# Sorted rows requested three tiles ahead, projection and norm as separate steps, and a walk that ends six experts sooner, in an attention-and-experts kernel

## The chip, the cores and the metric

The kernel runs on 1 core of one Trainium2 chip. The metric is device time in microseconds (us), the median of several executions. A core has five engines with a queue of instructions each: TensorE (PE in the profile), VectorE (DVE), ScalarE (ACT), GpSimd (POOL) and SyncE (SP). Each takes its instructions in the order in which the program has them, so an instruction that waits holds up all that stand behind it on its engine. DMA transfers are started from the queues of SP, ACT and POOL.

## The reference, cut to what matters

The input x is (2, 1024, 256) in float32. Each row of 256 is normed to xn. Two things are computed from xn, and the output is x plus both.

```
x  = L0_attn_x
xn = _layernorm(x)
out = x + attention(xn) + ffn(xn)

# attention: tokens of 16 channels in a 256 x 64 grid; two branches of 8 channels,
#   windows of 8 in one direction each: softmax(q k / sqrt(8)) v, plus a 3x3 depthwise conv of v
att    = concat(branch0, branch1) @ proj_w + proj_b
normed = (att - mean) * rsqrt(var + 1e-5) * ln_w + ln_b      # over 16 channels
att    = transpose(tokens + normed)

# ffn: 16 experts of 176 hidden units; every one of the 2048 rows goes to 6 of them
logits -> sigmoid -> choice of 2 of 4 groups, then of 6 experts, weights scaled by 2.5
out_row = sum over its 6 experts of  w * (silu(row @ g_e.T) * (row @ u_e.T)) @ d_e.T
          + a shared expert of 352 units
```

## The kernel before

**Stages.** The first 85 us or so load x and the weights, norm the rows (L223 to L249), choose the experts, sort the 2048 rows by which experts they go to, and run the shared expert in between (`shared_steps`, L266). The normed rows, with their 16 weights behind them, lie in DRAM as `xw_d`. The rest of the run interleaves two things.

**The experts.** The sorted rows stand in 16 tiles of 128 (`NTL`). `sorted_tile(t)` (L817) fetches tile t: an indirect DMA on POOL's queue gathers its rows into `xg` (three buffers), TensorE transposes them (L823), ACT copies them to `xsT` (L824), and DVE copies their 16 weights to `wsrt` (L826) and works out the six weights of the tile (L834 to L837). A buffer of `xg` is free again when both the transposes and L826 have read it. Every tile meets six experts, and there are 14 extra lists of rows for pairs that the six don't cover. One expert on one tile is a *slot*, and two slots are a *unit*. A slot's part on the way up (`up`, L851) is two matmuls L855 (four passes in the profile), a Silu on ACT (L857) and a multiply on DVE (L858, `hms`). The product's PSUM tile `pr_u` has three buffers. A unit's part on the way down is three transposes L869, a copy L871, and the matmuls L881 (six experts) or L889 (extras). When a tile's six experts are summed, ACT copies the sum to `ysum` (L1035; extras L1042), and POOL adds its rows to the output by an indirect DMA (L996, a *scatter-add*). There are 30 of these. Because they all add to the same output tensor, each one waits for the transfer before it.

**The attention.** `attention_steps` (L1049) yields its work as steps. There are four blocks (two batches, two halves of the columns), and each has: copies of rows (L670), eight projections (L675, each with four copies on ACT, L677 to L680), four products and sums on DVE (L688, L692), the softmax (L698 to L704), four weighted products and sums (L709, L714), two divides (L722), and eight transposes back (L729) with two copies into `oT` (L731). After the blocks come the last projections and their norms, `attended(g, h, xe, att)` (L765), eight times: four matmuls `pp` (L781), a copy with bias on ACT (L784), four transposes `pa` (L787), square (L791), variance (L793), root (L794), reciprocal (L795), multiply (L796), and on POOL a multiply and two additions into `att` (L797, L802). ACT loads a table for the root and another one for the Silu of the next expert. After each second g, `attention_added` (L1062) adds `att` to the output by four transfers from POOL's queue (L1065).

**What sets the order.** The loop at L1107 goes through the units. In each slot it fetches sorted tiles that are due (L1110), starts an expert, finishes an earlier one, and then calls `walked()` (L1082), which takes steps of the attention as long as they are behind the pace. Each step carries two costs, one for DVE and one for TensorE:

```python
of_slot = {"six": (0.5, 2.0), "extra": (0.8, 2.5)}
END = 72
pace = (whole[0] - LEAD - END * of_slot["six"][0] / of_slot["six"][1]) / (whole[1] - END)
...
while step and done[0] <= pace * done[1]:
    step[2]()
    counted(step)
    last, step = step, next(walk, None)
    if last[1] > 1:
        break
```

`END` is the TensorE time, in these costs, that is to be left when the attention is through. This gives the order in which the program states its work; a scheduling layer below it then moves single instructions within each engine's queue before the program is built.

Of the kernel before, what the change touches and what calls it, by code (L numbers as in the profile page):

```python
# [41 lines left out]
NTL = ROWS // P  # L42
# [9 lines left out]
def csw_block_moe(ctx: ExitStack, tc: tile.TileContext, x, qkv_w, conv_w0, conv_b0, conv_w1, conv_b1,  # L52
# [33 lines left out]
    def by_hl(t):  # L86
        return t.rearrange("(p l) d -> p l d", l=16)
# [135 lines left out]
    def statistics(g):  # L223
        st = small.tile([P, 4, 6], F32, name="st")
        mv = small.tile([P, 4, 2], F32, name="mv")
        for l in range(4):
            nc.vector.bn_stats(out=st[:, l, :], in_=xx[:, 4 * g + l, 0:W])
        for l in range(4):
            nc.vector.bn_aggr(out=mv[:, l, :], in_=st[:, l, :])
        rs = small.tile([P, 4], F32, name="rs")  # L230
        nc.scalar.activation(rs, mv[:, :, 1], AF.Sqrt, bias=eps)
        return mv, rs
# [84 lines left out]
    def meanwhile(until):  # L317

        while spent[1] is not None and spent[0] + spent[1] <= until:
            spent[0] += spent[1]  # L320
            spent[1] = next(share)
# [77 lines left out]
    for g in range(4):  # L399
        now, held = held, statistics(g + 1) if g < 3 else None  # L400
# [361 lines left out]
            nc.vector.tensor_copy(below[:, :, :, 0], pairs[:, 0:4, h, :, 1])  # L762
        return xe

    def attended(g, h, xe, att):  # L765

        if not last_room:
            last_room.extend(work.tile([P, 2, TB], F32, tag="f1024", name=name, bufs=3) for name in ("xr", "a", "sq"))
        xr = last_room[0].rearrange("p l (k d) -> p (l k) d", d=W)
        quarters = [t[:, n] for t in last_room[1:] for n in range(2)]  # L770
        a_, sq_ = quarters[(2 * g + h) % 3], quarters[3]
        if h == 0:
            nc.gpsimd.dma_start(out=xr, in_=by_hl(xw_d[0:ROWS, :])[:, 4 * g : 4 * g + 4, 0:W])

        pp = ps_m.tile([P, 4, P], F32, tag="m", name="pp")
        terms = [(lp[:, 0], xnT[:, h, 4 * g : 4 * g + 4, :]),
                 (lp[:, 1], xnT[:, h, 4 * g - 4 : 4 * g, :] if g > 0 else xe[0][:, h]),
                 (lp[:, 2], xnT[:, h, 4 * g + 4 : 4 * g + 8, :] if g < 3 else xe[1][:, h]),
                 (wp, oT[:, g, h])]
        for n, (l_, r_) in enumerate(terms):  # L780
            nc.tensor.matmul(pp.rearrange("p l q -> p (l q)"), lhsT=l_.rearrange("p t c -> p (t c)"),  # L781
                             rhs=r_.rearrange("p l q -> p (l q)"), start=(n == 0), stop=(n == len(terms) - 1))
        aT = a_.rearrange("p (l q) -> p l q", l=4)
        nc.scalar.activation(aT, pp, AF.Identity, bias=pbc)  # L784
        pa = ps_m.tile([P, 4, P], F32, tag="m", name="pa")
        for l in range(4):
            nc.tensor.transpose(pa[:, l, :], aT[:, l, :], ident)  # L787
        rows_a = pa.rearrange("p l (t c) -> p (l t) c", c=C)
        wide = [P, 32, C]
        sq, a = (t.rearrange("p (n c) -> p n c", c=C) for t in (sq_, a_))  # L790
        nc.scalar.activation(sq, rows_a, AF.Square)  # L791
        var = small.tile([P, 32], F32, tag="var", name="var")
        nc.vector.tensor_reduce(out=var, in_=sq, axis=AX.X, op=ALU.add)  # L793
        nc.scalar.activation(var, var, AF.Sqrt, bias=eps, scale=1.0 / C)  # L794
        nc.vector.reciprocal(var, var)  # L795
        nc.vector.tensor_tensor(a, rows_a, var.unsqueeze(2).to_broadcast(wide), ALU.mult)  # L796
        nc.gpsimd.tensor_tensor(a, a, lw.unsqueeze(1).to_broadcast(wide), ALU.mult)  # L797
        for m in range(2):
            to = att[m].rearrange("p n (l d) -> p n l d", d=16)[:, :, 4 * g : 4 * g + 4, 8 * h : 8 * h + 8]
            one = a.rearrange("p (l t) c -> p c l t", t=8)[:, 8 * m : 8 * m + 8]  # L800
            two = xr.rearrange("p l (t c) -> p c l t", c=C)[:, 8 * m : 8 * m + 8, :, 8 * h : 8 * h + 8]
            nc.gpsimd.tensor_tensor(to, one, two, ALU.add)  # L802
# [11 lines left out]
    w6 = route.tile([P, NTL * TOPK], F32, name="w6")  # L814
    st_ = {}

    def sorted_tile(t):  # L817
        xg = work.tile([P, ROW], F32, tag="xg", name="xg", bufs=3)
        nc.gpsimd.indirect_dma_start(out=xg, out_offset=None, in_=xw_d[:, :],  # L819
                                     in_offset=bass.IndirectOffsetOnAxis(ap=of[:, t : t + 1], axis=0))  # L820
        px_ = ps_m.tile([P, 2, P], F32, tag="m", name="px_")
        for h in range(2):
            nc.tensor.transpose(px_[:, h, :], xg[:, P * h : P * h + P], ident)  # L823
        nc.scalar.copy(xsT[:, t], px_)  # L824
        w = wsrt[:, t]
        nc.vector.tensor_copy(w, xg[:, W:ROW])  # L826

        if t > 1 and t % 2 == 0:
            return
        n = 1 if t < 2 else 2  # L830
        ts = slice(t + 1 - n, t + 1)
        wf = small.tile([P, 2, TOPK, E], F32, tag="wf", name="wf", bufs=1)[:, 0:n]
        wide = [P, n, TOPK, E]
        nc.vector.tensor_tensor(wf, e6b[:, ts].unsqueeze(3).to_broadcast(wide),  # L834
                                row_f.unsqueeze(1).unsqueeze(1).to_broadcast(wide), ALU.is_equal)
        nc.vector.tensor_tensor(wf, wf, wsrt[:, ts].unsqueeze(2).to_broadcast(wide), ALU.mult)
        nc.vector.tensor_reduce(out=w6.rearrange("p (t k) -> p t k", k=TOPK)[:, ts], in_=wf, axis=AX.X, op=ALU.add)  # L837
# [209 lines left out]
    att = []  # L1047

    def attention_steps():  # L1049
        for b in range(B):  # L1050
            for h in range(2):
                yield from attention(b, h)
        xe = []
        yield 0.6, 0.0, lambda: xe.extend(edges())
        att.extend(work.tile([P, 8, W], F32, tag=tag, name="att") for tag in ("prod", "qk"))
        for g in range(4):
            for h in range(2):
                yield 1.4, 3.9, lambda: attended(g, h, xe, att)
            if g % 2:
                waiting.extend([lambda m=m, b=b, n=g // 2: attention_added(m, b, n) for m in range(2) for b in range(B)])  # L1060

# [6 lines left out]

    of_slot = {"six": (0.5, 2.0), "extra": (0.8, 2.5)}
    of_tile = (0.75, 0.25)  # L1070
    END = 72
    in_walk = [4 * (16 * 2.3 + 3.3 + 2.5 + 1.5 + 1.4) + 0.6 + 8 * 1.4, 4 * 6.2 + 8 * 3.9]
    LEAD = 12
    done = [float(-LEAD), 0.0]
    whole = [in_walk[n] + NTL * TOPK * of_slot["six"][n] + NL * of_slot["extra"][n] + NTL * of_tile[n] for n in range(2)]
    pace = (whole[0] - LEAD - END * of_slot["six"][0] / of_slot["six"][1]) / (whole[1] - END)

# [1 line left out]
        for n in range(2):  # L1079
            done[n] += cost[n]  # L1080

    def walked():  # L1082
        step = held_.pop()
        while step and done[0] <= pace * done[1]:
            step[2]()
            counted(step)
            last, step = step, next(walk, None)
            if last[1] > 1:
                break
        held_.append(step)  # L1090

    walk = attention_steps()
    held_ = [next(walk)]
    sorted_tile(0)
    sorted_tile(1)
    walked()
    meanwhile(100)
    tiles_sorted = 2
    laid_out = list(units())
    begun_, hT_ = {}, {}  # L1100
# [6 lines left out]
    for u in range(len(laid_out) + 2):  # L1107
        for q in range(2):
            i = 2 * u + q
            while tiles_sorted < NTL and 5 * (tiles_sorted - 2) <= 6 * (i - 1):  # L1110
                sorted_tile(tiles_sorted)
                counted(of_tile)
                tiles_sorted += 1
            if i in (2, 4, 8) or i >= 14:
                next(extras_ if i < 14 else lists_, None)
            if u + 1 < len(laid_out) and laid_out[u + 1][0] == "extra":
                n = laid_out[u + 1][1] + q
                ahead[n] = gathered(lists[:, n : n + 1])
            if u < len(laid_out):
                if q == 0:  # L1120
                    fetched(u)
                begun_.setdefault(u, []).append(begun(laid_out[u], q, hms[:, u % 2]))
            if q == 1:
                if 0 <= u - 1 < len(laid_out):
                    hT_[u - 1] = hidden(hms[:, (u - 1) % 2])
                if 0 <= u - 2 < len(laid_out):
                    finished(laid_out[u - 2], hT_.pop(u - 2), wts[:, (u - 2) % 3], begun_.pop(u - 2))
            counted(of_slot[laid_out[min(u, len(laid_out) - 1)][0]])
            walked()
            if done_:  # L1130
                to_out(*done_.pop(0))
            while waiting:
                waiting.pop(0)()
# [8 lines left out]
    with tc.For_i(0, count_, 1) as n:  # L1142
# [5 lines left out]
        xg = gathered(to[:, 0:1])  # L1148
# [58 lines left out]
```

## Time and profile before

| | |
|---|---|
| median of the 3 runs | 453.98 us (453.94 to 454.08) |
| the profiled execution | 454.73 us |
| its span, first to last instruction | 453.0 us |
| mean granted TensorE clock | 0.976 |
| TensorE busy | 396.2 us, 87% of the span |
| DVE busy | 292.2 us, 65% |
| ACT busy | 215.2 us, 48% |
| POOL busy | 189.1 us, 42% |
| L855, up matmuls of the sorted rows | 132.0 us, 384 of 476 ns |
| L996, the 30 scatter-adds on POOL | 51.3 us, 1711 ns each |
| L819, the 16 gathers of sorted rows | 19.3 us, 1204 ns each |

How to read it: a row of digits shows the span in 40 slices of 11.3 us, each digit the busy share in tenths (9 is 90% or more). In a timeline a line gives the start, the time, the engine, the line of the kernel, the operation with output and input, and in brackets how long the engine had stood idle before it and what it waited for. The chain of waits follows the run back from its last instruction, at each step to what released it. A busy TensorE is not one at its peak, since the ends of its matmuls are modelled; the clock that it was granted is shown beside it.

### The profile page before, as it was taken

Reading aid. Unit: us, or ns where it says so; the run is one execution under the profiler, and the core shown is the slowest. Engines: PE = TensorE matmul, PEld = TensorE weight load, DVE = VectorE, ACT = ScalarE, POOL = GpSimd, SP = SyncE. Lnnn points to the kernel's source line nnn. Section 1 sums busy time; section 2 is a strip of 40 time slices with the busy share of each in tenths; the row PEclk is TensorE's granted clock in tenths of the full one; section 3 lists DMA queues with packets and bytes.
Section 4 is the critical chain, followed back from the end, with each engine's and each line's share of the span. In section 5 each row is a group of like instructions: output and inputs, shape, how many; then the busy total and the mean of one; then the engine's idle time right before and its main releaser. Section 6 shows DMA issues by size and latency. Waiting matters only on the chain.

```text
span 453.0 us, 6294 instructions
## 1 busy us (share of the span) xinstructions
PE 396.2 (87%) x1668; PEld 248.4 (55%) x1669; DVE 292.2 (65%) x515; ACT 215.2 (48%) x535; POOL 189.1 (42%) x207
## 2 busy tenths in 40 slices
PE   0999999998896978989799979899999899979990
PEld 0445465656464745656566646656666555447670
DVE  4627958689896945899838989469997223331210
ACT  2945248363372337253345363373623657773330
POOL 7300000322335151976832434505436274789331
PEclk9999999999898989999999999999999999998996
DMA  8999841322232100211122234202332101923922
GB/s 235 344 326 308 228 156 34 67 74 32 69 87 44 38 20 6 38 32 31 27 52 44 52 50 70 48 27 40 58 84 60 32 14 56 114 61 71 120 42 24
DMA packets 40178, 37.56 MB, mean 83 GB/s; under 512 B 5300, under 2 KB 37616, under 8 KB 40112
## 3 DMA queue, kind: packets, MB, share of 16 engines
q0 software_dynamic: 11616, 13.52, 18.5%
q1 hardware_dynamic: 27472, 22.59, 16.7%
q10 hardware_dynamic: 1056, 1.05, 0.7%
q8 instruction: 15, 0.25, 0.2%
q14 instruction: 19, 0.16, 0.1%
HBM read 27.70 MB, written 12.45 MB: 89 GB/s over the span
## 4 chain that ended last, share of the span: by engine, by line
PE 40%; DVE 24%; DMA 12%; issue 8%; POOL 7%; ACT 6%; POOLq 0%; SPq 0%; DVEq 0%; ACTq 0%
PE pr_u L855 9%; PE pr_y L881 5%; DVE pv L709 5%; DVE pr L688 4%; DVE s L692 4%; PE pg L275 4%; DMA out_dram<-ysum,lists 4%; PE pp L781 4%; PE py L290 4%; DVE o L714 4%; PE pu L275 4%; DMA out_dram<-att 4%; DVE hms L858 3%; PE pq L675 3%; DMA xg<-xw_d,lists 3%
## 5 line engine op out<-in xcount | busy, mean ns | idle before, releaser
L855 PE MATMUL pr_u<-w1s,xsT 128*128 x384 | 132.0, 476 | 2.4 <-DVE hms L858 1.9
L855 PEld LDWEIGHTS pr_u<-w1s,xsT 128*128 128x128 f32 x384 | 70.5, 193 | 39.0 <-issue 8.2
L996 POOL DMA_INDIRECT out_dram<-ysum,lists x30 | 51.3, 1711 | 88.3 <-ACT ysum L1035 36.1
L857 ACT ACTIVATE sg<-pr_u 128x176 f32<-128x176 f32 x110 | 34.5, 317 | 79.0 <-PE pr_u L855 72.7
L858 DVE SCALAR_TENSOR_TENSOR hms<-sg,w,pr_u 128x176 f32<-128x176 f32 x96 | 36.9, 389 | 44.2 <-ACT sg L857 42.6
L688 DVE TENSOR_TENSOR pr<-qk 128x2048 f32<-128x2048 f32 x16 | 36.6, 2287 | 15.6 <-ACT qk L677 10.9
L709 DVE TENSOR_TENSOR pv<-s,v 128x2048 f32<-128x2048 f32 x16 | 36.6, 2285 | 3.2 <-ACT s L700 3.1
L957 POOL TENSOR_SCALAR ysum<-row_h,spot 128x128 f16<-128x128 f16 x26 | 27.9, 1102 | 25.2 <-PE rows_of L948 15.0
L293 POOL DMA_DIRECT2D out_dram<-ysum x4 | 3.7, 921 | 78.7 <-ACT ysum L291 78.7
L692 DVE TENSOR_REDUCE s<-pr 128x256 f32<-128x2048 f32 x16 | 36.5, 2279 | 0.1
L714 DVE TENSOR_REDUCE o<-pv 128x256 f32<-128x2048 f32 x16 | 36.4, 2274 | 0.0
L869 PE MATMUL ph<-ident,hms 128*128 128x128 f32 x165 | 30.3, 281 | 6.1 <-ACT hT L871 3.6
L869 PEld LDWEIGHTS ph<-ident,hms 128*128 128x128 f32 x165 | 21.8, 145 | 24.1 <-issue 8.0
L982 POOL DMA_INDIRECT xg<-xw_d,lists x14 | 20.1, 1437 | 23.9 <-DVE hms L858 15.5
L881 PE MATMUL pr_y<-w2a,hT 128*128 x96 | 29.1, 386 | 0.0
L881 PE MATMUL pr_y<-wts,hT 128*128 128x256 f32 x96 | 28.9, 384 | 0.0
L881 PE MATMUL pr_y<-w2b,hT 112*128 x96 | 28.9, 382 | 0.0
L855 PE MATMUL pr_u<-w1s,xd 128*128 x56 | 21.4, 507 | 7.3 <-ACT xd L991 7.3
L871 ACT COPY hT<-ph 128x384 f32<-128x384 f32 x55 | 26.4, 480 | 2.1 <-PE ph L869 1.5
L675 PE MATMUL pq<-wq,rows 128*128 128x384 f32 x64 | 24.6, 501 | 3.1 <-ACT oT L731 2.0
L819 POOL DMA_INDIRECT xg<-xw_d,lists x16 | 19.3, 1204 | 18.6 <-PE pr_u L855 6.7
L290 PE MATMUL py<-room 128*128 128x256 f32 x96 | 23.9, 388 | 1.7 <-DVE room L284 1.7
(403 smaller groups left out, 713.1 us busy)
## 6 DMA issues: line engine op xcount, KB each, us to landing
w1s<-in_w_dram SPq DMA_DIRECT2D x22, 256.0 KB
wts<-in_w_dram SPq DMA_DIRECT2D x55, 64.0 KB
wts<-in_w_dram SPq DMA_DIRECT2D x55, 48.0 KB
xw_d<-xx SPq DMA_DIRECT2D x4, 544.0 KB
w2a<-in_w_dram SPq DMA_DIRECT2D x4, 512.0 KB
out_dram<-ysum POOLq DMA_DIRECT2D x4, 512.0 KB
xr<-xw_d POOLq DMA_DIRECT2D x4, 512.0 KB
out_dram<-att POOLq DMA_DIRECT2D x8, 256.0 KB
```

Of the source, the lines that this page charges most:

```text
L275: nc.tensor.matmul(ps, lhsT=w1h[:, half, h, P * m : P * m + P], rhs=xnT[:, h, 4 * k : 4 * k + 4, :].rearrange("p l q -> p (l q)"), start=( ...
L290: nc.tensor.matmul(py, lhsT=hms[k, m][:, P * c : P * c + P], rhs=w2h[:, m], start=(m == 0), stop=(m == 2))
L675: nc.tensor.matmul(pq.rearrange("p s t c -> p (s t c)"), lhsT=rows[:, i], rhs=wq.rearrange("p s t c -> p (s t c)"), start=True, stop=True)
L688: nc.vector.tensor_tensor(pr, q_.unsqueeze(3).to_broadcast(full), k_.unsqueeze(2).to_broadcast(full), ALU.mult)
L692: nc.vector.tensor_reduce(out=s[:, n : n + NW], in_=held.pop(n), axis=AX.X, op=ALU.add)
L709: nc.vector.tensor_tensor(pr, s[:, n : n + NW].unsqueeze(3).to_broadcast(full), v[:, br, m : m + NW].unsqueeze(2).to_broadcast(full), ALU. ...
L714: nc.vector.tensor_reduce(out=o[:, n : n + NW], in_=held.pop(n), axis=AX.X, op=ALU.add)
L855: nc.tensor.matmul(pu, lhsT=lhs[:, h, :], rhs=w1s[:, :, h, bass.ds(e * I, I)], start=(h == 0), stop=(h == 1))
L858: nc.vector.scalar_tensor_tensor(hm[:, 0:I], sg, w, pu[:, 1, :], op0=ALU.mult, op1=ALU.mult)
L869: nc.tensor.transpose(ph[:, s, :], units[:, P * s : P * s + P], ident)
L881: nc.tensor.matmul(py, lhsT=l_, rhs=r_, start=start and n == 0, stop=stop and n == 2)
L996: nc.gpsimd.indirect_dma_start(out=out_rows, out_offset=bass.IndirectOffsetOnAxis(ap=index, axis=0), in_=ys, in_offset=None, bounds_check= ...
```

## The change

Three edits. The first splits `sorted_tile`: a new function `asked()` starts the gather of the next tile, and `sorted_tile(t)` uses a gather that was started earlier. Three gathers are started ahead of the loop, and in each slot the loop starts more until three tiles beyond the sorted ones are asked for. The number of buffers of `xg` stays at three. With it the start of the interleaved part has another order: the projections of the first block are stated between the first and the second sorted tile, the remainder of the shared expert before the next steps of the walk, and each later tile is due one slot later (`i - 2` for `i - 1`).

The second edit splits `attended` into `attended` (loads, L781, L784) and `normed` (from the transposes on), as two steps with costs of their own, so that other work can stand between them. The third sets `END` from 72 to 84: the pace is higher, and the walk is through 12 us of planned TensorE time, six experts of 2.0, sooner.

```diff
-    def attended(g, h, xe, att):
+    def attended(g, h, xe):
...
         nc.scalar.activation(aT, pp, AF.Identity, bias=pbc)
+        return xr, a_, sq_
+
+    def normed(g, h, att, xr, a_, sq_):
+        aT = a_.rearrange("p (l q) -> p l q", l=4)
...
-    def sorted_tile(t):
+    asked_for = []
+    def asked():
+        t = len(asked_for)
         xg = work.tile([P, ROW], F32, tag="xg", name="xg", bufs=3)
         nc.gpsimd.indirect_dma_start(out=xg, out_offset=None, in_=xw_d[:, :],
                                      in_offset=bass.IndirectOffsetOnAxis(ap=of[:, t : t + 1], axis=0))
+        asked_for.append(xg)
+
+    def sorted_tile(t):
+        xg = asked_for[t]
...
-                yield 1.4, 3.9, lambda: attended(g, h, xe, att)
+                now = []
+                yield 0.1, 3.45, lambda: now.extend(attended(g, h, xe))
+                yield 1.3, 0.45, lambda: normed(g, h, att, *now)
...
-    END = 72
+    END = 84
...
-    LEAD = 12
+    FIRST_ROWS, LEAD = 2.5, 12
...
-    def walked():
+    def walked(until=None):
         step = held_.pop()
-        while step and done[0] <= pace * done[1]:
+        while step and done[0] <= (pace * done[1] if until is None else until):
...
+    for _ in range(3):
+        asked()
     sorted_tile(0)
+    walked(FIRST_ROWS - LEAD)
     sorted_tile(1)
+    meanwhile(100)
     walked()
-    meanwhile(100)
...
-            while tiles_sorted < NTL and 5 * (tiles_sorted - 2) <= 6 * (i - 1):
+            while tiles_sorted < NTL and 5 * (tiles_sorted - 2) <= 6 * (i - 2):
                 sorted_tile(tiles_sorted)
                 counted(of_tile)
                 tiles_sorted += 1
+            while len(asked_for) < min(NTL, tiles_sorted + 3):
+                asked()
```

## The prediction

> **What bounds it now.** I read the page first, then the waits, then the chain, then single stages. The profiled execution took 454.73 us for a span of 453.0 (1.73 lies around it); the median shown is 453.98, 0.75 lower. All sums below are made against the span; the difference is then taken from the median.
>
> ```profile
> PE 396.2 (87%) x1668; PEld 248.4 (55%) x1669; DVE 292.2 (65%) x515; ACT 215.2 (48%) x535; POOL 189.1 (42%) x207
> PE   0999999998896978989799979899999899979990
> DVE  4627958689896945899838989469997223331210
> ```
>
> TensorE is nearly always busy, but not alone: the DVE row shows four dense stretches, one for each attention block, with holes between them. Inside a block DVE's big products (2.3 us each) set the pace; in the holes and after the last block TensorE does. The waits of the first block, from the timelines of PE and DVE (start, duration, instruction, idle time before it and its releaser):
>
> ```profile
> 116.14 0.41 PE L823 MATMUL px__1148<-ident,xg 128*128 128x128 f32 x2 [1.65 <-DMA xg<-xw_d,lists]
> 141.26 0.50 PE L823 MATMUL px__1384<-ident,xg 128*128 128x128 f32 x2 [3.83 <-DMA xg<-xw_d,lists]
> 124.79 0.17 DVE L826 COPY wsrt<-xg 128x16 f32<-128x16 f32 x1 [2.02 <-DMA xg<-xw_d,lists]
> 141.15 0.18 DVE L826 COPY wsrt<-xg 128x16 f32<-128x16 f32 x1 [1.76 <-DMA xg<-xw_d,lists]
> 143.32 0.40 DVE L858 SCALAR_TENSOR_TENSOR hms<-sg,w,pr_u 128x176 f32<-128x176 f32 x1 [2.00 <-ACT sg L857]
> ```
>
> Gathered rows arrive late; the 2.00 is the same stall once more, since TensorE stood still for 3.83. The end of the run is a third regime, the chain of waits there:
>
> ```profile
> 419.11 7.99 DMA out_dram<-att
> ...
> 427.90 3.97 DMA out_dram<-ysum,lists
> ...
> 432.63 3.80 DMA out_dram<-ysum,lists
> ...
> 437.19 2.68 DMA out_dram<-ysum,lists
> ...
> 440.62 3.81 DMA out_dram<-ysum,lists
> ```
>
> Every addition to the output waits until the one before it has landed. TensorE ends at 441.07, yet the last scatter-add is issued at 445.19 (five stand behind the attention's own additions), and the span ends 7.81 later. So the time is: first last-projection on TensorE (L781, 352.96) plus 100.0. I predict both pieces.
>
> **The walk ends six experts sooner.** In the built programs 156 expert matmuls of the sorted rows stand ahead of the first L781 before, 144 after; two make an expert, so six fewer. In the clean tail a pair of experts takes 4.00 (424.36 to 428.36 from transpose to transpose), so 2.0 each: **12.0 us** of TensorE work leaves the front. Do the holes let it? From the last divide to the next block's first product DVE had 11.6 us (163.49 to 175.04), 11.8 (227.10 to 238.91), 12.1 (286.60 to 298.73). What has to happen in one is transposes 1.04, two copies 1.94, four projections of about 0.92 each on ACT and handovers: some 8. One to two experts, 2 to 4 us, come out of each of three holes, so they fit. The last hole (346.41 to 352.96) is 6.5, with about 4 needed.
>
> **Rows asked for three tiles ahead.** There are still three buffers, and POOL's queue before already holds ten gathers in a row, so the request itself moves little; what changes is the order on DVE and TensorE: each tile is turned about one expert later, and the copy L826 of tile 8 no longer stands ahead of the first weighted product. I followed the new order by hand from these rows: product or sum 2.28 (2.2 apart), hms 0.39 (0.31 apart), top and subtract 1.2 each, expert on TensorE 1.19, turn 0.22, gather issue 1.0 and landing 3.2 (94.16 to 97.41) to 5.5 (110.59 to 116.14) after issue. First product: 98.5 (was 99.07). A loss: the shared part's last multiply L284 now stands behind a second product, at 105.4 (was 103.60), so its projections L290 wait some 2.6 instead of 1.71. First weighted product 124.0 (was 126.35), second 133.2 (136.12), third 142.8 (146.44), after new waits of 1.9 and 0.6 for tiles 13 and 14, whose gathers stand behind the first scatter-add in POOL's queue (TensorE meanwhile waits some 3.1 for tile 8, which costs DVE nothing). Last divide about 160 (was 163.49). So 0.55 + 5.8 - 2.5, **3.9** of DVE time. Then the pair lists: TensorE waited 3.14 at L948 and 1.32 for oT; now the transposes come before L948, and I get 1.5 + 1.2 + 1.3. Nearly nothing, 0.4 taken. Together **4.3**; bounds: 0, if each old wait has a new one, and 7, if tiles 13 and 14 arrive in time (third product at 141.2) and L948's wait is covered.
>
> One gather in that stretch took 3.13 to issue, beside a product of DVE (136.12); others took 0.95. The Trainium skill (SBUF — State Buffer, Who interferes with whom) says that a DVE instruction with two SBUF inputs contends with a GpSimd instruction that reads SBUF. By that rule each gather beside a product loses some 2 us, and two more of them would turn the 4.3 into about 0, an estimate that meets rival 1. The trace agrees so far: the gather at 94.16, with no product beside it, took 0.98.
>
> **Projections and norms apart.** Same instructions: 8 times four L781 (3.43 us a step), four transposes. Before, each pa L787 waited for ACT's L784: 0.45, 0.34, 0.27, 0.25, 0.25, 0.25, 0.66, together 2.5 up to the last (402.30). Now a whole expert (1.19) stands between, and ACT needs 0.69 and handovers, so 2.3 of it goes. But the stretch holds more: before 5.5 sorted experts, 9 transposes and 10 down matmuls, now 6, 12 and 13; 0.6 + 0.3 + 1.3 = 2.2. First L781 to last pa stays 49.3. The 2.21 at 407.61 (xd) also goes; costed at nothing, since the adds' chain covers it.
>
> **The tail.** Last pa to POOL's last att: square 0.6, expert and gate 1.1, table 1.28, root 0.32, reciprocal and multiply 1.2, POOL a 1.27 and att 2.1, with handovers 8.7. Before it took 14.0 (402.95 to 416.95), because three scatter-adds stood between the att steps in POOL's queue, each behind the transfer before; now one does, and the step ahead is given 8.6 us more by an extra expert. Then 10.95 to the first add (416.95 to 427.90). Now **eight** adds follow, not five: intervals 4.73, 4.56, 3.43, 4.57 give about 31.0 for seven (bounds 24, all at 3.43, and 33, all at 4.73). Then 7.81. Sum from the first L781: 49.3 + 0.5 + 8.7 + 11.0 + 31.0 + 7.8 = 108.3, less 0.5 for the transposes counted in the first term: **107.8**, against 100.0. TensorE needs 12.0 more behind the first L781 than the 88.1 before, less some 4 of waits: 96, plus 0.4 and 7.8 is 104; so the adds still end last.
>
> **Sum.** -12.0 - 4.3 + 7.8 = **-8.5**: span 444.5, median 445.5.
>
> After the idle 1.65 the granted clock was 0.69 in the next 4 us (116 to 120), after 3.83 it was 0.68, after 1.71 and 2.10 it stayed 1.00. The Trainium skill (TensorE: Matmul & The Clock Gate, Part 1: The HAM clock gate) has the half clock come after about 3.4 us of idling in a free-running window; the trace shows less to be enough. By the rule the new waits (2.6, 1.5, 3.1 for tile 8) cost no clock, by the rows up to two times 1.3; in that block DVE leads, so the sum is the same.
>
> **Rivals.**
> 1. *The request is no earlier* (the change does not do what it says): three buffers, released by the same DVE copies, so the block's waits come back elsewhere and 4.3 becomes 0. For: POOL waited 6.30 and 2.50 for buffers, not for its turn. Against: 5.8 of DVE waits have lost their place in the order. -12.0 + 7.8 = -4.2: 449.8. Chance 0.18.
> 2. *DVE sets the walk, not TensorE* (slower): the experts taken out of the holes come back as DVE holes, because the next block's products wait for projections on ACT or lag inside blocks; DVE was busy 97% from 300 to 345. The first L781 is then only 4 sooner, while three more adds and 12 us of experts stand behind it: -4 + 7.8 = +3.8, 457.8. It decides from the point where the first L781 comes less than 7.8 us sooner, later than 345.2. Against: DVE had 47 us idle from 100 to 352, most of it in the holes. Chance 0.20.
> 3. *The adds run faster* (intervals of 3.4 where lists are short, or the attention's transfers land earlier) and TensorE's end decides: 104 in place of 107.8, so -12.0 - 4.3 + 4 = -12.3: 441.7. Chance 0.10.
>
> The forecast has 0.48; the last 0.04 lies within 0.2% of before, which is about what this measurement can tell from no change. Faster by more: 0.48 + 0.18 + 0.10 = 0.76; same 0.04; slower 0.20. Range 440 to 455: rival 3 and a gain of 7 in the first block below, rival 1 and half of rival 2 above.
>
> **What would show it.** Right: first L781 near 336.6; xg waits of the first block under 3 us on DVE; the last divide of block one near 160; no waits of pa for L784; eight scatter-adds 4.4 apart behind the last att transfer, the last near 437, and TensorE done about 4 us before it. Wrong: a first L781 later than 345, holes of DVE still over 11 us, or a chain that ends on TensorE.

## The result, and the profile after

Before and after were run in turn on one chip: 454.03 us before (median of 4), **448.34 us** after (447.56 to 448.94, 4 runs). The ratio is 0.9868, 95% interval 0.9845 to 0.9891, so the change takes off 4.9 to 7.0 us, 1.1 to 1.6%. The forecast was 445.5: the sign and the range held, the gain was 5.7 and not 8.5. Rival 1's number (449.8) lies nearer than the forecast's, though its mechanism did not act in the way that was said (below). The profiled execution took 448.94 us, its span is 447.2, 5.8 under the one before. From the page of the kernel after:

```profile
span 447.2 us, 6291 instructions
PE 393.4 (88%) x1668; PEld 247.4 (55%) x1669; DVE 293.0 (66%) x515; ACT 215.6 (48%) x535; POOL 187.8 (42%) x207
PE   0999999997887979898898899999899999999970
DVE  4627958679997948979779599398992333322110
PEclk9999999998999999999999699999999999999995
```

The dense stretches of DVE stand closer together. Between a block's last divide and the next first product DVE now has 7.9, 8.1 and 8.8 us (160.17 to 168.08, 218.75 to 226.83, 279.26 to 288.10) where it had 11.6 to 12.1. New is the 6 in the clock's row, at some 250 us. The first block's waits, from the timelines of PE and DVE; of the lines named here L823, L826 and L858 of before are L835, L838 and L870 after:

```profile
119.17 0.41 PE L835 MATMUL px__1182<-ident,xg 128*128 128x128 f32 x2 [1.37 <-DMA xg<-xw_d,lists]
125.68 0.41 PE L835 MATMUL px__1248<-ident,xg 128*128 128x128 f32 x2 [1.28 <-DMA xg<-xw_d,lists]
138.55 0.41 PE L835 MATMUL px__1371<-ident,xg 128*128 128x128 f32 x2 [1.72 <-DMA xg<-xw_d,lists]
140.90 0.40 DVE L870 SCALAR_TENSOR_TENSOR hms<-sg,w,pr_u 128x176 f32<-128x176 f32 x1 [1.05 <-ACT sg L869]
142.31 0.17 DVE L838 COPY wsrt<-xg 128x16 f32<-128x16 f32 x1 [1.01 <-DMA xg<-xw_d,lists]
```

DVE waits 1.05, 1.01 and 0.20 (142.94) here, 2.3 where it was 5.8 before; the last divide ends at 160.17 (before 163.49). The end of the chain of waits, whose view now reaches back only to 417.94:

```profile
422.71 3.76 DMA out_dram<-ysum,lists
...
427.23 3.64 DMA out_dram<-ysum,lists
...
431.62 2.70 DMA out_dram<-ysum,lists
...
435.08 3.78 DMA out_dram<-ysum,lists
...
439.92 1.24 POOL out_dram L1008
```

It is the chain of before with more links: eight scatter-adds behind the attention's own additions, from 408.88 to 439.61, each waiting for the landing of the one before. TensorE is done at 433.35.

Cut into the pieces of the forecast, the profiled runs of all kernels stand as follows (us; experiments in the next section; "adds" is their number behind the attention's last additions and the time from the first to the last issue; the time from the last pa to the last att is called the att chain below; a profiled execution lies up to 1.7 us from the median of its kernel):

| kernel | first L781 | last pa done | last pa to last att | to first add | adds | to the end | span |
|---|---|---|---|---|---|---|---|
| before | 352.96 | 402.95 | 14.0 | 11.0 | 5, 17.3 | 7.8 | 453.0 |
| after | 338.59 | 387.90 | 10.1 | 10.9 | 8, 30.7 | 7.6 | 447.2 |
| sooner_alone | 342.28 | 392.70 | 12.2 | 10.7 | 8, 31.0 | 7.9 | 454.4 |
| apart_alone | 353.30 | 402.58 | 17.5 | 11.8 | 5, 17.1 | 7.6 | 456.6 |
| rows_alone | 349.94 | 399.92 | 14.1 | 10.5 | 5, 16.9 | 7.7 | 449.1 |
| end_72 | 349.88 | 399.15 | 17.1 | 11.4 | 5, 17.2 | 7.7 | 452.5 |
| sooner_apart | 340.68 | 389.99 | 10.4 | 10.6 | 8, 30.1 | 7.8 | 448.8 |
| norms_on_dve | 338.78 | 388.60 | 6.3 | 11.5 | 8, 29.9 | 7.9 | 444.2 |
| dve_and_lists | 332.80 | 383.06 | 6.3 | 11.0 | 8, 30.1 | 7.7 | 438.2 |

So the miss lies mostly ahead of the first L781: 14.4 sooner, not 16.3. A wait that the forecast does not have stands there, and it makes the 6 in the clock's row. Timelines of DVE, POOL and PE, after:

```profile
241.85 0.18 DVE L977 SCALAR_TENSOR_TENSOR lists<-rows_of,ysum 128x26 int32<-128x26 f32 x1
241.94 2.29 DVE L688 TENSOR_TENSOR pr<-qk 128x2048 f32<-128x2048 f32 x1
242.50 2.64 POOL L994 DMA_INDIRECT xg<-xw_d,lists  x1 [0.30 <-issue]
247.04 0.69 PE L1001 MATMUL px__2528<-ident,xg 128*128 128x128 f32 x2 [3.09 <-DMA xg<-xw_d,lists]
248.37 0.47 PE L1001 MATMUL px__2549<-ident,xg 128*128 128x128 f32 x1 [0.64 <-DMA xg<-xw_d,lists]
```

Before:

```profile
234.48 0.18 DVE L965 SCALAR_TENSOR_TENSOR lists<-rows_of,ysum 128x26 int32<-128x26 f32 x1
234.94 1.05 POOL L982 DMA_INDIRECT xg<-xw_d,lists  x1 [6.37 <-DVE lists L965]
```

The lists of the extra rows are ended at a fixed expert. Before, that expert fell into a hole of DVE (227.10 to 238.91): the lists were written at 234.48, the gather was issued at once, and the transposes at 248.83 found their rows. After, the third block begins before that expert: the list's last matmul is issued at 235.68, but its step waits in DVE's queue behind a product and its sum (236.75 to 241.54), the gather's issue lies beside the next product and takes 2.64, and TensorE stands for 3.09 and 0.64. The windows of 4 us behind it (start:end, length, PE, PEld, DVE, ACT and POOL busy, granted clock, DMA share, GB/s) show what follows:

```profile
246.00:250.00 4.00, 2.19 (x5) 1.25 (x6) 3.39 (x4) 0.37 (x1) 1.36 (x2) 0.61 0.36 95
250.00:254.00 4.00, 3.75 (x9) 1.89 (x9) 0.40 (x1) 2.25 (x4) 0.94 (x1) 0.54 0.00 0
```

The clock is 0.61 and 0.54 for 8 us. DVE, which leads inside a block, then stands twice:

```profile
252.07 0.40 DVE L870 SCALAR_TENSOR_TENSOR hms<-sg,xg,pr_u 128x176 f32<-128x176 f32 x1 [2.65 <-ACT sg L869]
254.71 2.29 DVE L709 TENSOR_TENSOR pv<-s,v 128x2048 f32<-128x2048 f32 x1 [2.24 <-ACT s L700]
```

The first is the late expert. The second is the attention itself: the input of its exponential (L700) is written at 249.43, but on ACT the Silu of the late expert (251.72), a copy of late rows (251.94) and the load of a table (252.33) stand ahead of it, and L700 starts at 253.62. From its first product to its last divide the third block takes 52.4 us, where it took 47.7 before.

### The profile page after: what moved, and what is told of

Same layout as the page of the kernel before. It is cut to its first block, busy times and chain, and to the rows that moved or that the text cites. A ratio compares the mean times of both kernels' runs of the same rounds, so it can differ in the third digit from the quotient of the medians.

```text
span 447.2 us, 6291 instructions
## 1 busy us (share of the span) xinstructions
PE 393.4 (88%) x1668; PEld 247.4 (55%) x1669; DVE 293.0 (66%) x515; ACT 215.6 (48%) x535; POOL 187.8 (42%) x207
## 3 DMA queue, kind: packets, MB, share of 16 engines
q10 hardware_dynamic: 1056, 1.05, 0.7%
## 5 line engine op out<-in xcount | busy, mean ns | idle before, releaser
L867 PE MATMUL pr_u<-w1s,xsT 128*128 x384 | 128.3, 468 | 2.7 <-DVE hms L870 2.1
L870 DVE SCALAR_TENSOR_TENSOR hms<-sg,w,pr_u 128x176 f32<-128x176 f32 x96 | 37.4, 392 | 49.1 <-ACT sg L869 46.6
L688 DVE TENSOR_TENSOR pr<-qk 128x2048 f32<-128x2048 f32 x16 | 36.6, 2288 | 15.8 <-ACT qk L677 15.3
L994 POOL DMA_INDIRECT xg<-xw_d,lists x14 | 21.2, 1512 | 26.2 <-DVE hms L870 23.7
L969 POOL TENSOR_SCALAR ysum<-row_h,spot 128x128 f16<-128x128 f16 x26 | 21.3, 825 | 23.4 <-PE rows_of L960 17.0
L827 POOL DMA_INDIRECT xg<-xw_d,lists x16 | 21.6, 1353 | 18.7 <-PE px__1007 L835 6.5
L290 PE MATMUL py<-room 128*128 128x256 f32 x96 | 25.3, 402 | 2.5 <-DVE room L284 2.5
```

The source lines that it names most:

```text
L290: nc.tensor.matmul(py, lhsT=hms[k, m][:, P * c : P * c + P], rhs=w2h[:, m], start=(m == 0), stop=(m == 2))
L688: nc.vector.tensor_tensor(pr, q_.unsqueeze(3).to_broadcast(full), k_.unsqueeze(2).to_broadcast(full), ALU.mult)
L867: nc.tensor.matmul(pu, lhsT=lhs[:, h, :], rhs=w1s[:, :, h, bass.ds(e * I, I)], start=(h == 0), stop=(h == 1))
L870: nc.vector.scalar_tensor_tensor(hm[:, 0:I], sg, w, pu[:, 1, :], op0=ALU.mult, op1=ALU.mult)
```

## The experiments

Each kernel was compared with the kernel before on its own chip. Times from different chips are set side by side by these ratios, and a difference in us is the ratio's distance from 1 times 454.

**The theory** going in: experts taken out of DVE's holes and better ordered sorted rows bring the front forward; a serial chain of additions on POOL, not TensorE, sets the end. **Rivals**: DVE sets the walk, so that a shorter walk brings nothing; the request is no earlier; TensorE's end decides.

### The request by itself

The kernel before was built with `asked()` and its three tiles ahead alone, with the old due slot (`i - 1`) and the old start. On each of the five engines its order of instructions is that of the kernel before, without a difference. The request in the source therefore does nothing here: POOL's queue already ran ahead as far as three buffers let it. What remains of the edit is the due slot and the start.

### One edit at a time

sooner_alone, the kernel before with

```diff
-    END = 72
+    END = 84
```

> The kernel before with END = 84 and nothing else. My theory (experts come out of the holes of DVE, then eight serial additions to the output end the run, 4.4 us apart): the first last-projection (before 352.96) 10 to 12 us sooner, near 342, the stretch behind it 9 to 10 longer (three more additions, 13.2, less about 4 of the longer att chain): 450 to 452 us. Rival, DVE sets the walk: first last-projection less than 6 sooner, 455 to 458 us. Rival, TensorE's end decides: -12 + 4, 446 us.

Measured: 456.17 us, ratio 1.0050 (1.0033 to 1.0066), **slower by 1.5 to 3.0**. The front came as expected, 10.7 sooner, so rival 2 (DVE sets the walk) falls, though the time lies in the 455 to 458 us that it named. The stretch behind it grew by 12.1, not by 9 to 10: 13.7 for three more additions, less only 1.8 of the att chain. In POOL's queue two scatter-adds still stood between the last att steps. The new wait for the extras was here too (3.03 and 0.87, at 251.38 and 252.69).

apart_alone, the kernel before with

```diff
-                yield 1.4, 3.9, lambda: attended(g, h, xe, att)
+                now = []
+                yield 0.1, 3.45, lambda: now.extend(attended(g, h, xe))
+                yield 1.3, 0.45, lambda: normed(g, h, att, *now)
```

> The kernel before with the last projections and their norms as two steps of the walk, END = 72, nothing else. My theory: the waits of pa for the bias step (2.5 us in all) go, the scatter-adds behind the attention's stay five; in the built order two of them stand ahead of the last att steps and not three, so the att chain behind the last pa falls from 14.0 to about 10 and the last add comes 3 to 5 us sooner: 449.5 to 452 us. Rival, the split buys nothing because its expert fills no wait that counts: 453 to 454.5 us.

Measured: 456.69 us, ratio 1.0049 (1.0031 to 1.0067), **slower by 1.4 to 3.0**; both the theory and its rival missed it. Last pa to last att is not 10 but 17.5. POOL's timeline of this kernel shows why:

```profile
400.77 1.69 POOL L1000 DMA_INDIRECT out_dram<-ysum,lists  x1 [3.21 <-ACT a L784]
404.75 1.55 POOL L1000 DMA_INDIRECT out_dram<-ysum,lists  x1 [2.29 <-DMA out_dram<-ysum,lists]
405.78 1.81 POOL L801 TENSOR_TENSOR sq<-sq,lw 128x512 f32<-128x512 f32 x1
407.67 2.10 POOL L806 TENSOR_TENSOR att<-sq,xr 128x256 f32<-128x256 f32 x2
410.07 0.85 POOL L773 DMA_DIRECT2D xr<-xw_d  x1 [0.30 <-POOL att L806]
```

Three att groups were still to come, and two scatter-adds stood ahead of all of them. The first has to wait for the attention's four additions (issued from 387.47 on; the releaser named, L784, is not one of its inputs), the second for the first. POOL idles for 5.5 in front of work that was ready: the input of L801 at 405.78 was written by 394.37. The load of xr for the last pair comes only at 410.07. In the kernel after, one scatter-add is left in that place, and it comes before the last pa:

```profile
382.53 1.66 POOL L1008 DMA_INDIRECT out_dram<-ysum,lists  x1 [3.58 <-DVE hms L870]
383.62 1.88 POOL L801 TENSOR_TENSOR sq<-sq,lw 128x512 f32<-128x512 f32 x1
385.57 2.08 POOL L806 TENSOR_TENSOR att<-sq,xr 128x256 f32<-128x256 f32 x2
387.96 0.83 POOL L773 DMA_DIRECT2D xr<-xw_d  x1 [0.30 <-POOL att L806]
```

rows_alone, the kernel after with END = 72 and one step for projections and norms:

> The changed kernel with END = 72 and the projections and norms in one step again: only the sorted rows' part is left. My theory: DVE's last divide of block one near 160 (before 163.49), first last-projection 3.5 to 4.5 sooner, tail as before: 449.5 to 450.5 us. Rival, the request is no earlier and waits move elsewhere: 453.5 to 454.5 us.

Measured: 452.42 us, ratio 0.9966 (0.9947 to 0.9986), faster by 0.6 to 2.4. Between the two expectations. Last divide at 159.89 and first L781 3.0 sooner, as the theory said, but 2.0 of this was there at the first product already (97.10, before 99.07); the profiled execution is one of the fastest of its kernel (450.83), so the 1.5 of the ratio is the better size.

turn_later_only, the kernel before with

```diff
-            while tiles_sorted < NTL and 5 * (tiles_sorted - 2) <= 6 * (i - 1):
+            while tiles_sorted < NTL and 5 * (tiles_sorted - 2) <= 6 * (i - 2):
```

> The kernel before with 6 * (i - 2) in place of 6 * (i - 1): each sorted tile is turned about one expert later, nothing is asked sooner, the start is as before. My theory (the order in which tiles are turned carries the gain, not the request): most of the gain of the sorted rows' part, 450 to 452 us. Rival (the request or the new start carries it): 453.5 us or more, since a tile turned later is only later.

Measured: 452.54 us, ratio 0.9962 (0.9944 to 0.9979), slightly above the range named, but the same as rows_alone. By the ratios the due slot alone gives what this edit gives alone; neither the request nor the new start is needed for it. Its profiled execution (454.12) is the slowest of its kernel, so the trace (first L781 at 352.01) doesn't show where the gain lies, and whether the start adds something beside the other two edits was not tried.

### Edits in pairs

> The kernel before with END = 84 and the split of projections and norms, the sorted rows as before. My theory (the two edits price each other through POOL's queue: alone each lets two or more scatter-adds stand between the last att steps, together one): first last-projection 10.5 to 11 sooner (near 342), last pa to last att 10 and not 12.2 or 17.5, eight adds behind: rest 108.5 to 109, so 451.5 to 452.5 us. Rival, the edits simply add up (+2.0 and +2.2): 457 to 458.5 us. Rival, the sorted rows carry the whole gain: 454 us or more.

Measured: 450.64 us, ratio 0.9941 (0.9919 to 0.9962): 1.7 to 3.7 **faster**, from two edits of which each alone is slower. The time is a little under the range; the pieces are near those expected: the first L781 at 340.68, some 1.5 sooner than said, the att chain 10.4, the rest 108.1. Not additive: the rival's 457 is ruled out.

> The changed kernel with END = 72: sorted rows' order and the split, the walk as long as before. My theory (what each edit costs is decided by which scatter-adds the built order puts between the last att steps; here two stand there as in the split alone, five behind): front 2 to 3.5 sooner than the kernel before, last pa to last att 17 and not 14: 453 to 455 us, nothing gained on the kernel before. Rival, the edits add up one by one: split +2.4, rows -1.7: 454.5 us (not told apart by the time, but by the chain, which would then be 14 to 15 long).

Measured: 455.68 us, ratio 1.0024 (1.0007 to 1.0041), and the att chain is 17.1, as the theory said and its rival did not (the time lies 0.7 above the theory's range). All six ratios together (S for END = 84, A for the split, R for the rows; S with R was not run):

| S | A | R | A+R | S+A | S+A+R |
|---|---|---|---|---|---|
| 1.0050 | 1.0049 | 0.9966 | 1.0024 | 0.9941 | 0.9868 |

END = 84 costs 2.3 us alone and is worth 7.1 beside A and R. The split costs 2.2 alone and is worth 4.9 beside S.

### What sets the end

no_att_adds, the kernel after in which the last four of the attention's eight additions to the output are left out:

```diff
-            if g % 2:
+            if g == 1:
                 waiting.extend([lambda m=m, b=b, n=g // 2: attention_added(m, b, n) for m in range(2) for b in range(B)])
```

> The changed kernel without the last four additions of the attention's output (those that move half of the columns; they are left out). My theory (the serial additions set the end, TensorE is done 6.3 before the last is issued): the scatter-adds begin at the last att, about 11 sooner, until they meet the pace of TensorE; the last is issued about 1.5 behind TensorE's end, and the time is 442 to 444 us. Rival, TensorE or the last scatter-adds' own data set the end: 447.5 us or more.

Measured: 445.80 us, ratio 0.9849 (0.9812 to 0.9886), between the two. On the ratios it can't be told from the kernel after (0.9845 to 0.9891). In the profile the mechanism is there: the first of the eight scatter-adds is issued at 397.59, 0.2 behind the last att, and the last ones wait for their data:

```profile
419.88 1.54 POOL L1008 DMA_INDIRECT out_dram<-ysum,lists  x1 [2.93 <-DMA out_dram<-ysum,lists]
426.03 1.54 POOL L1008 DMA_INDIRECT out_dram<-ysum,lists  x1 [4.60 <-ACT ysum L1047]
432.95 1.54 POOL L1008 DMA_INDIRECT out_dram<-ysum,lists  x1 [5.38 <-ACTq L1162]
```

The last is issued 0.7 behind TensorE's end (432.27), 6.7 sooner than in the kernel after. But the span ends 10.2 behind it and not 7.6, so that 4.0 of span are gained in this pair of profiled runs, 1.1 of it ahead of the first L781 (337.51). What the 2.6 are is open.

norms_on_dve, the kernel after with

```diff
-        nc.gpsimd.tensor_tensor(a, a, lw.unsqueeze(1).to_broadcast(wide), ALU.mult)
+        nc.vector.tensor_tensor(a, a, lw.unsqueeze(1).to_broadcast(wide), ALU.mult)
...
-            nc.gpsimd.tensor_tensor(to, one, two, ALU.add)
+            nc.vector.tensor_tensor(to, one, two, ALU.add)
```

> The changed kernel with the norm's last multiply and its two additions on DVE in place of POOL. My theory (the chain from the last pa through the att steps to eight serial additions ends the run): last pa to last att falls from 10.1 to 5.5 to 7, all behind it moves up as much: 444.5 to 446 us. Rival, DVE's extra work holds up the experts and TensorE's end (433.35) decides: 447.5 to 450 us.

Measured: 445.39 us, ratio 0.9812 (0.9780 to 0.9844), as expected; its interval lies just below that of the kernel after, and the gain over it is 2.5 by the ratios. Last pa to last att is 6.3 where it was 10.1, and the eight scatter-adds behind it moved up by 2.5 to 3.4, not by the whole 3.8; TensorE is done at 434.05, later than without the edit (433.35). POOL's timeline:

```profile
394.74 4.82 POOL L1079 DMA_DIRECT2D out_dram<-att  x4 [9.95 <-DVE att L806]
406.41 1.66 POOL L1008 DMA_INDIRECT out_dram<-ysum,lists  x1 [6.85 <-ACT hT L883]
```

So the chain through the att steps and the serial additions sets the end of the kernel after, and TensorE does not.

end_72_dve, the same with END = 72:

> The changed kernel with END = 72 and the norm's last multiply and additions on DVE. My theory (a walk that is not shortened lost its gain only because POOL's queue put two scatter-adds between the last att steps): last pa (399.2) to last att falls from 17.1 to 6.5 to 8, the load of xr now being what stands behind those scatter-adds; first of five scatter-adds near 418, the last near 435.5, TensorE done by 433: 443.5 to 446 us, about 10 under the same kernel with the steps on POOL, where the same edit at END = 84 took 3 to 4. Rival, the edit on DVE is worth the same anywhere: 451.5 to 453 us. Rival, TensorE ends later without the waits that now overlap: 447 us or more.

Measured: 449.68 us, ratio 0.9914 (0.9883 to 0.9945). A miss of the theory by 4, and of the first rival too. The second rival, 447 or more because TensorE ends later, has it right: TensorE ended at 439.23, not 433 (432.43 in end_72). The att chain fell from 17.1 to 10.4, not to 8. The two scatter-adds are still in POOL's queue (395.55 and 399.48), ahead of the load of xr (400.48), and now another engine waits for that load:

```profile
405.97 1.08 DVE L806 TENSOR_TENSOR att<-a,xr 128x256 f32<-128x256 f32 x2 [6.70 <-DMA xr<-xw_d]
```

Behind this instruction in DVE's queue stands the multiply of an expert (L870), and TensorE waits 3.43 for it (at 407.41; its clock is 0.57 from 407 to 411). The queue blocks as the theory has it; moved work carries the block onto another engine.

### The new wait for the extras

lists_sooner, the kernel after with

```diff
-            if i in (2, 4, 8) or i >= 14:
-                next(extras_ if i < 14 else lists_, None)
+            if i in (2, 4, 8) or i >= 13:
+                next(extras_ if i < 13 else lists_, None)
+            if i in (20, 26, 32):
+                next(lists_, None)
```

> The changed kernel with the lists of the extras ended four experts sooner (begun one expert earlier, three of its steps two to an expert), so that the lists' last step stands ahead of a product of DVE and the first extras' gathers are asked at the same expert but find DVE's lists ready. My theory: TensorE's waits of 3.09 and 0.64 for those rows at 247 go, and with them 1 to 2.5 us of the front: first last-projection 336 to 337.5, time 445.5 to 447.5 us. Rival, DVE leads that block and the waits cost nothing: 448 to 448.7 us.

Measured: 447.05 us, ratio 0.9859 (0.9833 to 0.9886); not told apart from the kernel after by the time. The first L781 came at 336.80, as the theory said. The waits at 247 are gone and the third block takes 56.07 from its first product to the next block's (after: 61.27), but the doubled steps brought waits of 2.83 and 1.98 at 160 to 166, and the third block began 3.4 later (230.23, after 226.83). Inconclusive by itself, hence the next.

dve_and_lists, norms_on_dve with three doubled steps that lie inside the second block:

```diff
             if i in (2, 4, 8) or i >= 14:
                 next(extras_ if i < 14 else lists_, None)
+            if i in (34, 37, 40):
+                next(lists_, None)
```

> The norm's last steps on DVE as in the run before it, and the extras' lists ended three experts sooner, the doubled steps all in the second attention block and none beside the turn from the first block to the second. My theory: TensorE's waits of 3.14 near 247 go and the first last-projection comes 1.5 to 3 sooner (336 to 337.5), the stretch behind it stays 105 to 106: 442 to 444 us. Rival, DVE leads the third block and the waits cost little: 445 to 446 us.

Measured: **440.54 us, ratio 0.9715 (0.9693 to 0.9738)**, 11.9 to 13.9 under the kernel before, and its interval lies below those of the kernel after and of norms_on_dve. More than expected: the first L781 is 6.0 sooner than in norms_on_dve, and the third block takes 56.06, not 61.60, while the stretch behind stays 105.4. From its page:

```profile
DVE  4626967679997966979949999398993665651110
PEclk9999999998999999999999999999999999999998
```

The 6 in the clock's row is gone. The lists are written at 221.83, ahead of the block's first product, and the gather behind them took 1.05. So the wait that the forecast lacks cost some 5 us: 4.4 by the ratios of these two kernels, 5.5 to 6.0 in their profiled runs, of which the one lies 0.6 above its median and the other 0.7 below. On TensorE it is the wait of 3.7 and about 3.4 lost at a low clock (8 us at 0.57).

dve_and_lists_96, the same with END = 96:

> The same with END = 96: four more experts fewer in the walk (156 expert matmuls of 222 ahead of the first last-projection, 164 before), ten scatter-adds behind the attention's own and not eight. My theory: front 5 to 8 sooner where DVE's holes still hold TensorE's work (5 us of idle DVE before the second block, 7 before the fourth), two more additions at 4.4 (8.8 later) behind it: no gain over END = 84, 443 to 446 us. Rival, TensorE's end decides and holes are work-free: 440 us or less. Rival, holes of DVE cannot shrink and the front gains under 3: 448 us or more.

Measured: 445.29 us, ratio 0.9787 (0.9765 to 0.9809), a time as the theory said, with less in front than it said. Four experts (8 us) fewer in the walk bring the first L781 only 3.8 forward (328.96), and ten additions stand behind. The last is issued at 436.16, TensorE ends at 435.48: the two ends have met, and the front has come near to what rival 2 spoke of.

## Why the prediction was right, and where it was wrong

**Sign and mechanism: right in the main.** The first L781 came well inside 345.2, DVE's holes shrank to about the 8 us counted as work, and serial additions set the end.

**The walk, 12.0.** The size held (10.7 alone, 11.3 from end_72 to after), but partly by luck: two misses go opposite ways. From the traces of before and after, the three holes and the stretch from the last divide to the first L781 shrank together by 14.3 (42.0 to 27.7; the last of them from 6.5 to 2.9, where the forecast counted about 4 as needed). The first block's last divide came 3.3 sooner, the second block took 1.4 less and the fourth 0.1, and the third took 4.7 more: together 14.4. The 4.7 is the stall at the extras: in dve_and_lists, without it, the third block takes 47.4. **The failed step is the question whether the holes let the experts go:** it counted what has to happen in a hole (transposes, copies, projections) and not what else had used it, the last step of the lists at 234.48 with its gathers. That row stood in the trace of before.

Without the stall, from end_72 (349.88) to dve_and_lists (332.80), the front comes 17.1 sooner: besides the 12 us of work, TensorE's waits of over 1 us ahead of the first L781 fall from 15.3 to 12.0, and the mean clock of the run rises from 0.969 to 0.991. The two kernels differ in the lists' steps too, and in the norms on DVE (all behind the first L781); a walk of END = 72 with the doubled steps was not run, so the 17.1 is not END's alone.

**Rows three ahead, 4.3.** The replay held in block one: last divide 160.17 (forecast about 160), DVE's xg waits 1.2 (under 3), the wait for L284 2.52 (2.6); the wait for tile 8 was 1.28, not 3.1. But the term was mis-sized: alone it gives 1.5 (0.6 to 2.4), beside the other two 3.3 (0.9941 to 0.9868). In the profiled runs it makes 3.0 of the front (352.96 to 349.94), so of the 1.9 that the front misses some 1.3 belong here and some 0.7 to the walk; the split is rough, for kernels with the same front (after, norms_on_dve, no_att_adds) differ by up to 1.3 in it. Of rival 1 the first half is true, the request moves no instruction, and 2.3 of the 5.8 of DVE's waits did come back; its price of 0 was wrong, since the due slot of the turns was part of the same edit.

Of the Trainium skill's rule on shared ports (SBUF — State Buffer, Who interferes with whom) the forecast said that two more gathers beside products would bring the term to about 0. The two came: three of that stretch took over 2 us (3.03 at 114.19, 2.49 at 125.03, 3.41 at 133.20), in rows_alone too (3.03, 2.45, 2.95). Before it was one, but not all others took 0.95 as the forecast has it: 1.52 at 110.59, beside the end of a product, and 1.80 at 120.97. The trace agrees with the rule, and the term fell, though not to 0; that these gathers are what it lost was not tried.

**Projections and norms apart, about 0.** First L781 to last pa was 48.7 (49.3), and only one wait of pa for the bias step is left (0.25 at 378.75). Before there were six and not seven, 2.2 in all and not 2.5. As an edit it was not nothing: +2.2 alone, -4.9 beside END = 84. Its price does not lie in TensorE's waits, where the forecast looked, but in which scatter-adds the built order puts between POOL's att steps. That the forecast read this order off the built program, and took one scatter-add there, is why the tail came out.

**The tail, 107.8.** Measured 108.6. Seven intervals 30.7 (31.0), last att to first add 10.9 (11.0), the end 7.6 (7.8). The att chain was 10.1, not 8.7: the load of xr stood behind the att step in POOL's queue (387.96) and the last pair waited 1.01 for it. TensorE was done 6.3 before the last issue (about 4 forecast).

**Sum:** front -14.4 (-16.3), rest +8.6 (+7.8), together -5.8 (-8.5).

## What to carry to other kernels

Before work is taken out of an engine's hole, list every step that lies in the hole, with who waits for its result: an idle stretch can be the place where a late, small step found the engine free. In-order queues that mix slow serial transfers with steps of a chain make edits interact: read the built order and price edits together, for two that each cost 0.5% alone took off 0.6% together. And where the end of a run is a serial chain, cutting the steps in front of it is worth most of what they take (3.8 out of the att chain gave 2.5 by the ratios), until another engine's end is met.

## What the runs showed of the hardware

A gather that is issued beside a product of DVE (two SBUF inputs) is done when the product is, plus 0.84 to 0.91, in all seven cases of the kernel after, of which four: 114.19 to 117.22 beside a product that ended at 116.31; 125.03 to 127.52, product to 126.68; 133.20 to 136.61, product to 135.76; 242.50 to 245.14, product to 244.23. Beside no product it takes 0.94 to 1.04 there, and so does one issued 0.62 ahead of a product (123.77, 0.96), while the one at 133.20, 0.29 ahead, is held. Since the end follows the product's end and not the issue, the gather looks not slowed but held until the product is over, and the price depends on how early in the product it comes.

TensorE's clock fell after idling of 2.52 (0.61 in 106 to 110 of the kernel after), 3.09 with 0.64 soon behind (0.57 over 8 us) and 3.43 (0.57 in 4 us, end_72_dve). The Trainium skill (TensorE: Matmul & The Clock Gate, Part 1: The HAM clock gate) names an idle window of some 3.4 us; 2.52 here, and 1.65 in the trace of before, were enough, so the measurement decides. But 1.72 in the kernel after (at 138.55) and 2.81 in norms_on_dve (at 104.98) left the clock at 1.00, so the length of a wait alone does not tell.

Additions of rows to one output follow each other every 4.4 us (3.5 to 4.8 in the kernel after), of which 2.7 to 3.8 are the transfer in the chain of waits. That interval, times the number of additions left when the rest is done, was the most reliable term of the forecast.
